# Four-layer graph network: adjacency products in a one-pass format behind a branch, the hyperedge sum one hyperedge at a time, x in DRAM

## The chip, the cores and the metric

The kernel runs on one core of one Trainium2 chip. The metric is the device time in microseconds (us) of one execution, and lower is better. The times given for a kernel are the median, the lowest and the highest of its runs. Besides these there is one execution under the hardware profiler; it has its own time and its own span, which is the time from the first to the last instruction. Engines are named as in the profile: PE is TensorE, DVE is VectorE, ACT is ScalarE, POOL is GpSimd, and SP is the engine that issues most of the transfers.

## The reference

The input x holds 8 batches of 2048 nodes with 64 features each. One adjacency matrix adj, 2048 x 2048 in fp32 with entries 0 and 1, is shared by all layers and batches. There are four layers, and each is x = x + layer(relu(layernorm(x))). H is 2048 nodes x 64 hyperedges, 0 or 1. What the layers compute, per batch:

```python
# layer 0: hypergraph attention and an adjacency mean
h = x @ W
s = leaky_relu(h @ a_node, 0.2)
alpha = softmax(where(H.T > 0, s[None, :], NEG), -1)       # 64 hyperedges x nodes
agg = alpha @ h                                            # 64 x 64 features
beta = sigmoid((h @ a_gn)[None, :] + (agg @ a_ge)[:, None])   # hyperedge x node
all_he = elu(beta[..., None] * h[None] + (1 - beta[..., None]) * agg[:, None])
industry = (adj / maximum(adj.sum(-1), 1)[:, None]) @ (x @ W_ind)
se = tanh(elu(agg) @ fcW + fcb) @ av                       # one score per hyperedge
coefs1 = softmax(where(H > 0, se[None, :], NEG), -1)       # node x hyperedge
g = einsum('ne,enf->nf', coefs1, all_he)                   # the sum over hyperedges
out = softmax-weighted mix of industry and g
# layer 1: Chebyshev terms x, A x, 2 A (A x) - x, with weights per node
#          from a 16-wide embedding
# layer 2: three times: effects = adj @ v; h = relu([v, effects] @ W1.T + b1);
#          v = h @ W2.T + b2
# layer 3: attention over all node pairs, scores multiplied by adj
```

The product adj @ something therefore occurs six times with all 8 batches side by side (512 columns): once in layer 0, twice in layer 1 and three times in layer 2.

## The kernel before

**Layouts.** Two batches of 64 features share the 128 partitions, so that an array is four tiles q = 0 to 3 of 128 x 2048 (features by nodes, "T form"), or sixteen tiles t of 128 nodes x 512 (batches and features, "node form"). `Halves` stores either form in two tiles with tags q0 to q7; a tag is one buffer of 2 MB (16 KB a partition), and an array that takes over a tag has to wait until the last reader of the former one is done. x itself stays in SBUF for the whole kernel as `self.x`, 4 MB, and `load_x` reads it from DRAM only in layer 0.

**Order.** The text is written in the order of the computation; the framework places semaphores and moves independent instructions of one engine past each other within what the buffers of the pools allow. All transfers of data are issued on SP in one queue, so that a transfer that has to wait for a buffer holds those behind it.

**Adjacency product** (`adj_product`, matmuls recorded under the helper `mm`, L57). Four chunks `ch` of 512 output nodes. In each, 16 source tiles m: a DMA brings two of them at once (`adj_t`, 512 KB), and for each of the four q one fp32 matmul of 128x128 by 128x512 adds to the accumulator `pp{q}` in PSUM. A chunk is 64 matmuls; `done` then empties the four accumulators. In layer 0 `each` adds up the rows of adj on GpSimd for the degree; in layer 1 `done` transposes the result back into node form, and `done2` runs the convolution (`pk`, `acc`, `po`); in layer 2 `done` runs the two small matrix products and the transposes (`to_nodes`).

**Sum over hyperedges** (`beta_and_weights`, then `hyper`). Partitions are (batch of the pair, hyperedge), and the loop runs over q and the 64 features f, 256 steps of 2048 nodes. h was split into three bf16 parts that were written to DRAM (`parts`) and come back as `mv`; `spread` copies one feature's row to all 128 partitions by matmuls with a 0/1 matrix `sel` into `pw`. `first_half` (L566, VectorE) forms z = (h - agg) * beta in two operations of 1024. `exponentials` (L574, L575, ScalarE) forms exp(z + agg) and relu(z + agg). `second_half` (L580, VectorE) forms y = min(exp, 1) + relu, which is elu plus 1, over 2048 columns, and four matmuls with `strip` sum y over the hyperedges with their weights `wt` into `acc`. `finish` collects the rows of a q.

**Layernorm** (`layernorm_relu`). Four chunks: a matmul with `center` subtracts the mean (`pc`, copied to `xc`), GpSimd squares, and two small matmuls give the variance (`pv`) and spread the inverse deviation (`pr`). `xc` has two buffers.

**Layer 3** (`attend`) has per batch and node tile an operation on GpSimd (L908) and two on VectorE (L911, L915) over 2048 columns, transposes (L928) and the product `po`.

## Time and profile before

| what | value |
|---|---|
| median of 3 runs | 5292.23 us (5259.44 to 5293.93) |
| the profiled execution, its time | 5293.93 us |
| its span | 5292.1 us |
| mean granted TensorE clock | 0.889 |
| busy: PE, PE weight loads | 4552.3 us (86%), 1832.7 us (35%) |
| busy: DVE, ACT, POOL | 2628.2 (50%), 1789.9 (34%), 945.0 us (18%) |
| DMA | 156.37 MB, mean 30 GB/s |

The order of the computation lets the span be cut into stages:

| stage | from, to (us) | length |
|---|---|---|
| start: layernorm, h, x_ind | 0 to 137.5 | 137.5 |
| layer 0, adjacency product | 137.5 to 386 | 248.5 |
| layer 0, attention of the hyperedges over nodes | 386 to 480 | 94 |
| layer 0, coefficients and sum over hyperedges | 480 to 1885 | 1405 |
| mix, layernorm of layer 1, transposes | 1885 to 2102 | 217 |
| layer 1, first product | 2102 to 2338 | 236 |
| layer 1, second product and convolution | 2338 to 3177 | 839 |
| layernorm of layer 2 | 3177 to 3253 | 76 |
| layer 2, three products | 3253 to 4055 | 802 |
| layer 3 | 4055 to 5292 | 1237 |

How to read the profile's lines. In the groups of instructions a line gives the source line, the engine, the operation, the tiles written and read, partitions x elements, and the number of instructions; then, after the bar, the busy time in us and the mean of one in ns; and after the second bar the engine's idle time just before them and what ended most of it. In the timeline a line gives the start in us, the duration in us, the engine, the line, the operation, its tiles and how many were joined in the line; in brackets stands the wait before it. In the table of windows a line gives the window, its length, and for each engine the busy time with the number of instructions, then the granted clock, the DMA share and the GB/s.

### The profile page before, as it was taken

How to read it: one execution, taken by the hardware profiler on the slowest of the kernel's cores; microseconds unless marked ns; L12 is line 12 of the kernel's file. 1: busy time of each engine (PE TensorE's matmuls, PEld its weight loads, DVE VectorE, ACT ScalarE, POOL GpSimd, SP SyncE). 2: the span in 40 equal slices, each digit the busy share in tenths (PEclk: the TensorE clock that was granted, in tenths of full speed). 3: DMA queues.
4: the chain of work that ended last, by engine and by line, in shares of the span. 5: the costliest groups of instructions: out<-in, count | busy, mean ns of one | idle time of the engine just before them, and what ended most of it. 6: DMA issues, size and time to landing. Idle time of an engine off the chain costs nothing.

```text
span 5292.1 us, 35768 instructions
## 1 busy us (share of the span) xinstructions
PE 4552.3 (86%) x14310; PEld 1832.7 (35%) x14374; DVE 2628.2 (50%) x2556; ACT 1789.9 (34%) x1652; POOL 945.0 (18%) x650
## 2 busy tenths in 40 slices
PE   8896566767566688999999999999999899999998
PEld 3333111111111122442323323444443455555555
DVE  3113898998989924003222232000002577777776
ACT  3002686886878832000000001000001244444444
POOL 4325000000000022004243241000001223232322
PEclk8997777677887788999999998999999798988898
DMA  2210000000000000230110101111110101010000
GB/s 81 92 56 0 3 6 5 5 5 5 6 3 0 0 24 28 72 100 12 48 25 24 32 0 57 60 63 64 61 64 16 40 5 36 5 36 5 28 5 5
DMA packets 76455, 156.37 MB, mean 30 GB/s; under 512 B 6464, under 2 KB 12736, under 8 KB 74112
## 3 DMA queue, kind: packets, MB, share of 16 engines
q1 hardware_dynamic: 76288, 154.07, 9.1%
q8 instruction: 113, 1.85, 0.1%
q14 instruction: 54, 0.44, 0.0%
HBM read 143.57 MB, written 10.49 MB: 29 GB/s over the span
## 4 chain that ended last, share of the span: by engine, by line
PE 56%; DVE 32%; POOL 7%; ACT 3%; issue 2%; DMA 1%; SPq 0%; POOLq 0%; DVEq 0%; ACTq 0%
PE pp L57 25%; DVE z_t L566 11%; PE po L57 9%; DVE e_t L580 7%; POOL acc L731 4%; PE pt L928 4%; PE p L57 4%; DVE e_x L580 3%; PE pd L57 3%; PE pk L57 3%; DVE m L915 3%; DVE y L730 2%; PE pr L57 2%; DVE m L911 2%; ACT m L920 1%
## 5 line engine op out<-in xcount | busy, mean ns | idle before, releaser
L566 DVE SCALAR_TENSOR_TENSOR z_t<-pw,agg_e,beta 128x1024 f32<-128x1024 f32 x512 | 636.9, 1279 | 38.1 <-PE pw L57 11.8
L575 ACT ACTIVATE z_t<-z_t,agg_e 128x2048 f32<-128x2048 f32 x256 | 512.7, 2003 | 8.2
L57 PE MATMUL po<-et,h_n 128*64 128x256 f32 x2048 | 511.6, 402 | 0.3 <-DVE st L919 0.3
L57 PE MATMUL pw<-mv,sel 128*128 128x512 bf16 x960 | 380.4, 497 | 120.3 <-DVE z_t L566 104.4
L57 PE MATMUL acc<-e_t,strip 128*32 128x512 f32 x1368 | 254.5, 810 | 232.5 <-DVE e_t L580 232.4
L57 PE MATMUL pp<-adj_t,v_a 128*128 128x512 f32 x1024 | 447.5, 592 | 0.0
L908 POOL TENSOR_SCALAR m<-ed,es 128x2048 f32<-128x2048 f32 x128 | 306.2, 2392 | 750.4 <-PE pt L928 421.7
L928 PE MATMUL pt<-ident,m 128*128 128x128 f32 x2048 | 357.6, 317 | 84.5 <-ACT m L920 50.2
L731 POOL TENSOR_TENSOR acc<-acc,y 128x512 f32<-128x512 f32 x224 | 282.7, 1262 | 814.6 <-DVE y L730 814.4
L574 ACT ACTIVATE e_t<-z_t,agg_e 128x2048 f32<-128x2048 f32 x171 | 342.4, 2002 | 181.2 <-DVE z_t L566 181.2
L580 DVE SCALAR_TENSOR_TENSOR e_t<-e_t,z_t 128x2048 f32<-128x2048 f32 x171 | 390.0, 2281 | 11.9 <-ACT z_t L575 11.9
L57 PEld LDWEIGHTS po<-et,h_n 128*64 128x64 f32 x2048 | 279.5, 144 | 195.4 <-issue 69.9
L915 DVE CUSTOM_DVE_ANT_0 m<-m,ar 128x2048 f32<-128x2048 f32 x128 | 345.7, 2701 | 2.2 <-POOL ar L873 2.2
L911 DVE SCALAR_TENSOR_TENSOR m<-ed,es,m 128x2048 f32<-128x2048 f32 x128 | 304.7, 2381 | 80.8 <-POOL m L908 80.8
L928 PEld LDWEIGHTS pt<-ident,m 128*128 128x128 f32 x2048 | 254.9, 158 | 256.2 <-ACT et L932 117.4
L932 ACT COPY et<-pt 128x512 f32<-128x512 f32 x384 | 215.2, 584 | 353.4 <-PE pt L928 353.0
L730 DVE TENSOR_TENSOR y<-pk,emb 128x512 f32<-128x512 f32 x224 | 154.8, 691 | 350.0 <-POOL acc L731 267.1
L63 ACT COPY xc<-pc 128x512 f32<-128x512 f32 x32 | 18.7, 585 | 914.4 <-PE pc L57 906.6
L920 ACT ACTIVATE m<-m,st 128x2048 f32<-128x2048 f32 x128 | 256.6, 2005 | 171.8 <-DVE st L919 171.8
L65 DVE COPY ef<-pp 128x512 f32<-128x512 f32 x24 | 16.6, 692 | 579.1 <-PE pp L57 567.6
L57 PEld LDWEIGHTS <-sel 128*128 128x128 bf16 x1024 | 98.2, 110 | 568.6 <-issue 530.5
L57 PE MATMUL pk<-x,w 64*128 64x512 f32 x512 | 286.8, 641 | 0.0
(250 smaller groups left out, 5441.1 us busy)
## 6 DMA issues: line engine op xcount, KB each, us to landing
adj_t<-in_adjT_dram SPq DMA_DIRECT2D x192, 512.0 KB
ar<-in_adj_dram SPq DMA_DIRECT2D x16, 1024.0 KB
xin<-in_xT_dram SPq DMA_DIRECT2D x8, 1024.0 KB
emb<-in_embT_dram SPq DMA_DIRECT2D x8, 1024.0 KB
parts<-part SPq DMA_DIRECT2D x16, 384.0 KB
mv<-parts SPq DMA_DIRECT2D x64, 96.0 KB
out_dram<-o SPq DMA_DIRECT2D x16, 256.0 KB
w<-in_wk_dram SPq DMA_DIRECT2D x6, 256.0 KB
```

The lines of the kernel that those rows point to most:

```text
L57: self.nc.tensor.matmul(out, lhsT, rhs, start=start, stop=stop)
L566: nc.vector.scalar_tensor_tensor(zs[i % 2][:, s], pws[i][c], agg_e[:, q, f : f + 1], beta(q)[:, s], op0=OP.subtract, op1=OP.mult,)
L574: nc.scalar.activation(es[i % 3], z, AF.Exp, bias=ag)
L575: nc.scalar.activation(z, z, AF.Relu, bias=ag)
L580: nc.vector.scalar_tensor_tensor(y, y, 1.0, zs[i % 2], op0=OP.min, op1=OP.add)
L730: nc.vector.tensor_mul(y, pk, emb[:, blk])
L731: nc.gpsimd.tensor_add(acc, acc, y)
L908: nc.gpsimd.tensor_scalar(m, ed, 0.2, es2[:, it, b : b + 1], op0=OP.mult, op1=OP.add)
L911: nc.vector.scalar_tensor_tensor(m, ed, es[:, it, b : b + 1], m, op0=OP.add, op1=OP.max)
L915: nc.vector.tensor_tensor_reduce(out=m, in0=m, in1=rows[i], op0=OP.mult, op1=OP.max, scale=1.0, scalar=-3.0e38, accum_out=st[:, 0:1],)
L920: nc.scalar.activation(m, m, AF.Exp, bias=st[:, 0:1], accum_out=st[:, 1:2])
L928: nc.tensor.transpose(pt[:, u], m[:, (t + u) * P : (t + u + 1) * P], ident)
```

## The change

The core of it:

```diff
+F12 = mybir.dt.float32r
...
+        dram = ctx.enter_context(tc.tile_pool(name="dram", bufs=1, space=bass.MemoryType.DRAM))
+        self.xs = [
+            [a["xT"][:, :, c * CW : (c + 1) * CW].rearrange("q p n -> p q n") for c in range(NC)]
+        ]
+        for i in range(3):
+            self.xs.append([dram.tile([P, NP, CW], F, name=f"x{i}_{c}") for c in range(NC)])
...
+    def exact(self, ap):
+        return ap.bitcast(F12) if self.short else ap
...
+    def split(self, dst, t, src, s=None):
...
+        self.nc.scalar.copy(hi.bitcast(F12), src)
+        self.nc.vector.tensor_sub(lo.bitcast(F12), src, hi)
...
+    def load_x(self, pool, layer, ch, bufs=None):
+        x = pool.tile([P, NP, CW], F, name="x_ch", bufs=bufs)
+        self.nc.sync.dma_start(x, self.xs[layer][ch])
+        return x
...
+    def store_x(self, layer, ch, x):
+        self.nc.sync.dma_start(self.xs[layer + 1][ch], x)
...
-                xc = w.tile([P, NP, CW], F, name="xc")
+                xc = w.tile([P, NP, CW], F, name="xc", bufs=1)
                 sq = w.tile([P, NP, CW], F, name="sq", bufs=1)
-                x = self.load_x(w, ch) if first else self.x[:, :, s]
+                x = self.load_x(w, layer, ch)
...
+                    moving = at[:, i]
+                    if self.short:
+                        moving = w.tile([P, CW], F12, name="adj_12", bufs=bufs)
+                        nc.scalar.copy(moving, at[:, i])
+                    for j, part in enumerate(src.parts):
+                        for q in range(NP):
+                            self.mm(
+                                out[q], self.exact(part(m)[:, q * P : (q + 1) * P]),
+                                moving,
+                                start=m == 0 and j == 0, stop=m == NT - 1 and j == 1,
+                            )
...
+    def check_adj(self, pool, slots):
...
+        nc, tc = self.nc, self.tc
+        rows = [slots.tile([P, 2, N], I32, name=f"rows{i}", tag=f"q{6 + i}") for i in range(2)]
+        seen = slots.tile([P, 2, N], I32, name="seen", tag="q8")
+        for t in range(NT):
+            row = rows[t // 2 % 2][:, t % 2]
+            nc.sync.dma_start(row, self.a["adj"][t * P : (t + 1) * P].bitcast(I32))
+            low = seen[:, 0] if t == 0 else row
+            nc.vector.tensor_scalar(low, row, LOW, None, op0=OP.bitwise_and)
+            if t > 0:
+                nc.vector.tensor_tensor(seen[:, 0], seen[:, 0], low, op=OP.bitwise_or)
...
+        top = pool.tile([P, 1], F, name="top")
+        nc.vector.tensor_reduce(top, seen[:, 0], axis=AX.X, op=OP.max)
+        flag = pool.tile([1, 1], I32, name="flag")
+        with tc.tile_pool(name="check_ps", bufs=1, space=PSUM) as ps:
+            pt = ps.tile([1, P], F, name="pt")
+            nc.tensor.transpose(pt, top, self.ident)
+            one = pool.tile([1, 1], F, name="one")
+            nc.vector.tensor_reduce(one, pt, axis=AX.X, op=OP.max)
+            nc.vector.tensor_scalar(flag, one, 0.0, None, op0=OP.is_gt)
+        return flag
...
+            self.layernorm_relu(0, write)
+            flag = self.check_adj(pool, slots)
...
+            with tc.tile_pool(name="h_ps", bufs=3, space=PSUM) as ps:
...
+        hn, h_t, h_n = self.h
...
+            w_ind = self.block_diag(k, a["W_ind"], "w_ind")
+            x_ind = Split(slots, "x_ind")
+            with tc.tile_pool(name="x_ps", bufs=3, space=PSUM) as ps:
+                for t in range(NT):
+                    pn = ps.tile([P, NP, P], F, name="pn")
+                    for q in range(NP):
+                        self.mm(pn[:, q], hn(q)[:, t * P : (t + 1) * P], w_ind)
+                    self.split(x_ind, t, pn.rearrange("n q f -> n (q f)"))
...
+            ind = Halves(slots, "ind", ("q0", "q1"), False)
...
+            beta = Halves(slots, "beta", ("q4", "q5"), False)
+            coef = Halves(slots, "coef", ("q6", "q7"), False)
...
+                for t in range(NT):
+                    mk = w.tile([P, 2, D], F, name="mk")
+                    nc.sync.dma_start(mk[:, 0], a["H"][t * P : (t + 1) * P])
...
+                    lg = w.tile([P, NB, D], F, name="lg")
+                    full = [P, NB, D]
+                    nc.gpsimd.tensor_mul(lg, se, mk[:, 0:1].to_broadcast(full))
+                    nc.gpsimd.tensor_add(lg, lg, mk[:, 1:2].to_broadcast(full))
+                    st = w.tile([P, 2, NB], F, name="st")
+                    nc.vector.tensor_reduce(st[:, 0], lg, axis=AX.X, op=OP.max)
+                    nc.vector.tensor_sub(lg, lg, st[:, 0].unsqueeze(2).to_broadcast(full))
+                    nc.scalar.activation(lg, lg, AF.Exp)
+                    nc.vector.tensor_reduce(st[:, 1], lg, axis=AX.X, op=OP.add)
+                    nc.vector.reciprocal(st[:, 1], st[:, 1])
+                    nc.vector.tensor_mul(lg, lg, st[:, 1].unsqueeze(2).to_broadcast(full))
...
+                        self.copy(coef.tiles[i][:, :, t * P : (t + 1) * P], pt[:, 2 * i : 2 * i + 2])
...
+            HW = 2 * CW
+            with (
+                tc.tile_pool(name="g", bufs=3) as w,
+                tc.tile_pool(name="g_ps", bufs=2, space=PSUM) as ps,
+            ):
+                for q in range(NP):
+                    acc = w.tile([P, N], F, name="acc", bufs=1)
+                    for e in range(D):
+                        pick = w.tile([P, 2, D], F, name="pick", bufs=2)
+                        nc.gpsimd.tensor_copy(
+                            pick, self.ident[:, e::D].unsqueeze(2).to_broadcast([P, 2, D])
+                        )
+                        pick = pick.rearrange("k s f -> k (s f)")
+                        ag = agg_t[:, q, e : e + 1]
+                        for c in range(N // HW):
+                            pb = ps.tile([P, HW], F, name="pb")
+                            pc = ps.tile([P, HW], F, name="pc")
+                            for pp, src in ((pb, beta), (pc, coef)):
+                                for i in range(2):
+                                    lo = c * HW + i * CW
+                                    self.mm(
+                                        pp[:, i * CW : (i + 1) * CW], pick, src(q)[:, lo : lo + CW]
+                                    )
+                            s = slice(c * HW, (c + 1) * HW)
+                            z = w.tile([P, HW], F, name="z")
+                            nc.vector.scalar_tensor_tensor(
+                                z, h_t(q)[:, s], ag, pb, op0=OP.subtract, op1=OP.mult
+                            )
+                            y = w.tile([P, HW], F, name="y")
+                            nc.scalar.activation(y, z, AF.Exp, bias=ag)
+                            nc.scalar.activation(z, z, AF.Relu, bias=ag)
+                            nc.vector.scalar_tensor_tensor(y, y, 1.0, z, op0=OP.min, op1=OP.add)
+                            if e == 0:
+                                nc.vector.tensor_mul(acc[:, s], y, pc)
+                            else:
+                                nc.vector.tensor_mul(y, y, pc)
+                                nc.gpsimd.tensor_add(acc[:, s], acc[:, s], y)
+                    nc.vector.tensor_scalar_add(h_t(q), acc, -1.0)
...
-                    xin = self.load_x(w, ch)
+                    x = self.load_x(w, 0, ch, bufs=2)
...
...
+        h_n = Split(slots, "h_n")
+        ah = Halves(slots, "ah", ("q4", "q5"), True)
...
+        ah_n = Split(slots, "ah_n")
+        for t in range(NT):
+            self.split(ah_n, t, ah(t))
...
+                two = slots.tile([P, 2, NP, CW], F, name="two", tag="q5")
+                x2, x = two[:, 0], two[:, 1]
+                nc.sync.dma_start(x, self.xs[1][ch])
...
+                self.store_x(1, ch, x)
+            self.adj_product(ah_n, w, ps, done2, bufs=3)
...
+        v_next = Halves(slots, "v_next", ("q2", "q3"), True)
...
+                v_n = Split(slots, "v_n")
+                for t in range(NT):
+                    self.split(v_n, t, v_next(t))
...
+                        x = self.load_x(w, 2, ch, bufs=1)
...
-                self.adj_product(bufs[step % 2], w, ps, done, bufs=6)
...
+                        self.store_x(2, ch, x)
...
+                self.adj_product(v_n, w, ps, done)
...
+                    x = self.load_x(w, 3, ic, bufs=1)
...
+                flag = kern.start(flags, slots)
+            long = tc.nc.values_load(flag, min_val=0, max_val=1)
...
+            with tc.If(long < 1) as check:
+                rest(True)
+            with check.Else():
+                rest(False)
```

**Products.** `short` is the arm of a branch in which `adj_product` copies each 512-column piece of adj on ScalarE into `adj_12`, of type float32r [...], and multiplies it by two parts of the features, `hi` (the features rounded by a ScalarE copy to that format) and `lo` (the rest, by a VectorE subtraction). A chunk then has 128 matmuls. `Split` holds the parts in q6 to q9. In the other arm adj stays fp32, and the two parts are multiplied as fp32.

**Check and branch.** `check_adj` reads all of adj as integers (16 transfers of 1 MB), keeps the low 12 bits of each (bitwise and), collects them (bitwise or), and forms a flag. The flag is read into registers, and layers 0 to 2 exist twice, in the two arms of `tc.If`. `start` (layernorm, check, h) stands ahead of the branch, the last layer behind it.

**Sum over hyperedges.** Partitions are now (batch of the pair, feature), as in T form, and the loop runs over q, hyperedges e and halves c of 1024 nodes: 512 half-steps. `pick` is built on GpSimd per (q, e); four fp32 matmuls with it spread the rows of beta (`pb`) and of the coefficients (`pc`). VectorE forms z from h_t (SBUF) and pb (PSUM), ScalarE forms exp and relu, VectorE forms y from two SBUF operands and multiplies it by pc, and GpSimd adds it to `acc` in SBUF. A new stage ahead of it ("coef") forms the softmax over hyperedges for each of the 16 node tiles and turns it into T form. `beta_and_weights` and `hyper`, the bf16 parts and their transfers are gone.

**x in memory.** `self.x` is gone; x lies in DRAM in four chunks a layer (`self.xs`), is loaded by `load_x` where it is used and stored by `store_x`. In `layernorm_relu` `xc` has one buffer. In layer 1 the second product has three buffers of adj_t instead of four, and `ah` keeps the first product in q4 and q5 until it is split. In layer 2 v_next takes q2 and q3, and adj_t has four buffers instead of six.

## The prediction

> **What bounds the kernel now.** I read the page's time slices, then a table of windows cut at the stages, then the chain of waits and the single instructions inside the two stages that change. The windows (us, then busy PE, weight loads, VectorE, ScalarE, GpSimd, clock, DMA share, GB/s):
>
> ```profile
> 137.50:386.00 248.50, 232.96 (x520) 101.92 (x520) 23.53 (x22) 0.00 (x0) 78.08 (x64) 0.96 0.24 74
> 480.00:1885.00 1405.00, 907.67 (x3375) 201.47 (x3439) 1243.11 (x875) 1039.33 (x534) 50.34 (x48) 0.76 0.01 4
> 2102.00:2338.00 236.00, 233.31 (x646) 104.94 (x645) 18.57 (x35) 14.87 (x33) 0.00 (x0) 0.98 0.25 75
> 2338.00:3177.00 839.00, 829.71 (x1664) 261.57 (x1664) 209.73 (x304) 0.00 (x0) 282.68 (x224) 0.99 0.10 29
> 3253.00:4055.00 802.00, 798.39 (x1944) 352.92 (x1942) 63.95 (x90) 55.06 (x88) 0.35 (x2) 1.00 0.18 59
> ```
>
> Lines 1, 3, 4 and 5 hold the six adjacency products (24 chunks): TensorE is busy nearly all the time and nothing else is. Line 2 is the sum over hyperedges: VectorE is full, TensorE is not. Inside these stages:
>
> ```profile
> L566 DVE SCALAR_TENSOR_TENSOR z_t<-pw,agg_e,beta 128x1024 f32<-128x1024 f32 x512 | 636.9, 1279 | 38.1 <-PE pw L57 11.8
> L580 DVE SCALAR_TENSOR_TENSOR e_t<-e_t,z_t 128x2048 f32<-128x2048 f32 x171 | 390.0, 2281 | 11.9 <-ACT z_t L575 11.9
> ...
> 3456.48 49.09 PE L57 MATMUL pp<-adj_t,v_a 128*128 128x512 f32 x114
> ...
> 700.58 0.59 PE L57 MATMUL pw<-mv,sel 128*128 128x512 bf16 x2 [0.32 <-DVE z_t L566]
> ...
> 4613.88 2.29 DVE L915 CUSTOM_DVE_ANT_0 m<-m,ar 128x2048 f32<-128x2048 f32 x1
> 4641.72 3.63 DVE L915 CUSTOM_DVE_ANT_0 m<-m,ar 128x2048 f32<-128x2048 f32 x1
> ...
> 4641.24 1.97 POOL L908 TENSOR_SCALAR m<-ed,es 128x2048 f32<-128x2048 f32 x1 [7.69 <-issue]
> ```
>
> An fp32 product is two MATMUL records; 114 of them in 49.09 us is 0.429 each, 0.858 a product. Two bf16 ones end in 0.59 although each lasts 0.377, so one pass takes 0.213. The last three lines matter most below: a VectorE operation with two SBUF inputs takes 2.29 us alone and 3.63 when a GpSimd operation holds until 4643.21; it then ends 2.1 us after GpSimd.
>
> [...]The pitch of 0.429 against a load of 0.190 (the LDWEIGHTS row of pp) agrees for the products; in the convolution it does not wholly: pairs start 1.055 apart instead of 0.858. [...]the masks row shows 1226 ns for 2048 elements, L580 2281.[...]
>
> **The change, part by part**, against the profiled execution (5293.9 us, span 5292.1; the runs' median is 5292.2). The taken arm is the short one, since adj holds zeros and ones only.
>
> *Products.* A chunk is 64 fp32 products (54.9 us); it becomes 128 one-pass ones. No row shows this format at 4 bytes. I take the bf16 pitch: 128 x 0.214 = 27.4, saving 27.5. [...]an uncovered load adds 0.1 (half of the convolution's 0.2 a product), and two passes would make it 0.429. ScalarE's new copies of adj (16 x about 0.6 = 9.6 a chunk), GpSimd's row sums (16 x 1.26 = 20.2) and DMA (4.2 MB in 27 us, 155 GB/s; 148 was moved in 98 to 137 us at a share of 0.45) stay under 27.4. By stage:
> - First layer: 4 x (27.4 + 6.0 at each boundary, the 3.36 us reciprocal and what surrounds it) = 134 for 248.5: -115.
> - Second layer, first product: 4 x (27.4 + 3 of transposes + about 2 until the four accumulators are emptied) + 2 = 132 for 236: -104.
> - Second product: 4 x 27.5 = -110. The split of ah frees q4, on which the embedding load waits on SP, and adj_t stands behind it there: +9. Sum -101.
> - Third layer: a chunk of 67.2 becomes 27.4 + 12 fp32 products (10.3) + 16 transposes (2.0) + 1.1 of waits for hh, which the built order fills with three to six one-pass matmuls. 12 x 40.8 + 3 splits begun late at 4 = 502 for 802: -300.
>
> *Sum over hyperedges.* 256 steps over features become 512 half-steps over hyperedges of 1024 columns. VectorE per half-step: z 1279 (the same operand kinds as L566), y 2281 - 1067 = 1214, the product with pc 691 + 533 = 1224 (512 columns more at 0.96 a ns): 3.72, or 3.47 when each overlaps its predecessor by 0.085, as L566's pairs do. TensorE: four fp32 products, 3.43. ScalarE: two of about 1.12. GpSimd: the add lies between 1262 (512) and 4513 (2048 columns, L299), 2.35, plus half a pick (a copy of 512 takes 0.61; about 0.3), together 2.5. The built order keeps VectorE two half-steps deep (y, the z two ahead, the product), so ScalarE's 2.3 us are covered. But y has two SBUF inputs and the add reads SBUF: 1.2 + 2.35 + 0.15 = 3.7 exclude one another. Three resources thus lie between 3.4 and 3.7; coupled in fixed order none is met exactly. Behind a held y stand z and the product on VectorE, and behind these TensorE's next pb and pc, which wait for the PSUM that they free. I take 3.8: 512 x 3.8 = 1946, plus 24 for four ends (the single acc must be drained, then one 2048 operation). Bounds: 3.47 (lock wholly hidden) and 4.22 (loads uncovered, 4 x 1.055).
> Before it, the coefficient stage: 16 tiles of about 3.8 us VectorE (four 128x512 operations of 0.69, 0.42 of copies, 0.6 small), 61, with GpSimd's 2 x 1.26 a tile in conflict with two of them, and 10 to fill: 78. Sum 2048 for 1405: +643.
>
> *Check, branch, start.* Sixteen ands (1.23 to 2.28 each), fifteen ors (2.29) and a reduction (2.28) are 56 to 73 us of VectorE among the 31 of the layernorm[...]. The layernorm's end moves from 79 to about 115; 16.8 MB more DMA fits beside it. The flag's short chain 5, then h 32 (32 us of TensorE, held behind the flag's transpose), [...]loads of w_ind behind it 5, x_ind 17: the product starts at 179, not 137.5: +42. The bf16 parts and their DMAs are gone, and this is inside that figure.
>
> *x in memory.* The loads after the mix wait on SP behind the last store: +10. Third layer's layernorm +3. Leaving the arm and reloading before the last layer +15. Elsewhere loads run 30 us ahead, and cost 7 (a 1 MB load took 5.2) where that cover is gone. xc has one buffer instead of two, so a chunk's first copies wait until the chunk before has read its last xc: 0 to 10 us a layernorm, by the 76 us that four chunks take now; I take 6 in each of these three.
>
> Sum: 42 - 115 + 643 + 16 - 104 - 101 + 9 - 300 + 21 = +111. 5293.9 + 111 = 5405.
>
> **Rivals.** A measurement of this kernel can tell about 1% from no change.
> - A, as summed: 5405, own range 5328 to 5518 (half-step 3.65 to 4.0). Chance 0.47. For it: the lock line above. Against: 3.47 is possible.
> - B, faster: the add runs exactly under z and the product, which have one SBUF input each, so the lock costs nothing and VectorE streams. Half-step 3.47: -169, 5236. It decides when z and the product (2.35) are as long as the add and y always asks first. The convolution speaks for it: y there (one SBUF input) takes 691 with and without the add beside it. Chance 0.17.
> - C, TensorE bounds the loop: pick's loads stay uncovered as in the convolution, 4.22: +215, 5620. Against: all tiles are 128x128, as in the products. Chance 0.13.
> - D, the lock the other way round: the add asks first, y waits for it whole, then z and the product run with GpSimd idle: 2.35 + 1.0 + 2.35 = 5.7. If a quarter of the half-steps do so, +243, 5648; all, +973, 6378. Against: y stands directly behind the product on VectorE, the add waits for its semaphore. Chance 0.08.
> - E, the format doesn't do what it says: 0.1 more per matmul, 24 x 128 x 0.1 = +307, 5712; two passes, 24 x 27.5 = +660, 6065. Chance 0.15.
>
> **How the numbers follow.** The likeliest case gives 5405. Range 5210 to 5735: it takes in B, C and E's first half and leaves out some 0.2. Faster by over 1% (below 5239): somewhat over half of B, and A where several of the other stages fall short, 0.15. Within 1%: B's rest and the low end of A, 0.15. Slower: 0.70.
>
> **What would show it.** In the profile after: one-pass pp records of about 0.38 with a pitch of 0.214, chunks of the third layer 41 apart; z, y and acc starting 3.8 apart, y longer than 1.21 and the add longer than 2.35 in some; the first product at about 179 and the mix at about 2455. Wrong if the pitch is over 0.25, if a half-step leaves 3.6 to 4.0, or if a stage outside these moves by over 20.

## The result, and the profile after

The changed kernel takes 5526.15 us (median of 4 runs, 5523.31 to 5539.47) against 5292.4 us: a ratio of 1.0462, 95% interval 1.0418 to 1.0506, so it is slower. The forecast was 5405, slower, with a range of 5210 to 5735. Direction and range hold; the loss is 234 us where 111 were summed, so the size does not hold. The profiled execution took 5524.61 us with a span of 5522.7 us; the differences below are of spans.

The stages, cut in the same way as before. The border between the two products of the second layer is put at the convolution's first matmuls in both kernels (2337.8 and 2812.5 us).

| stage | before | after | change | the prediction's term |
|---|---|---|---|---|
| start | 137.5 | 158.8 | +21 | +42 |
| first layer, product | 248.5 | 151.8 | -97 | -115 |
| attention of the hyperedges | 94 | 92.1 | -2 | 0 |
| coefficients and sum over hyperedges | 1405 | 2021.8 | +617 | +643 |
| mix, layernorm, transposes | 217 | 230.3 | +13 | +16 |
| second layer, first product | 236 | 157.7 | -78 | -104 |
| second product and convolution | 839 | 870.9 | **+32** | **-101** |
| layernorm of the third layer | 76 | 86.8 | +11 | +9 |
| third layer, products | 802 | 501.7 | -300 | -300 |
| last layer with what leads to it | 1237 | 1250.8 | +14 | +21 |
| sum | 5292 | 5522.7 | +231 | +111 |

One row is off by 133 us. The others are off by 13 together, the other way; that is in part luck, since four of them are off by 18 to 26 each and cancel in pairs. The windows that answer to those of before (window, length, busy PE, weight loads, VectorE, ScalarE, GpSimd, clock, DMA share, GB/s):

```profile
158.80:310.60 151.80, 130.04 (x520) 101.26 (x521) 28.57 (x26) 37.21 (x60) 64.91 (x52) 0.93 0.31 97
402.70:2424.50 2021.80, 1864.07 (x4192) 776.57 (x4192) 1929.08 (x1667) 1215.16 (x1082) 1598.91 (x791) 0.98 0.00 1
2654.80:2812.50 157.70, 150.74 (x721) 114.16 (x721) 35.26 (x72) 67.27 (x134) 0.00 (x0) 0.90 0.40 120
2812.50:3683.40 870.90, 854.06 (x1664) 287.14 (x1665) 209.41 (x304) 39.36 (x64) 283.02 (x224) 0.83 0.13 38
3770.20:4271.90 501.70, 498.22 (x1973) 352.10 (x1971) 91.20 (x133) 193.80 (x323) 0.28 (x2) 1.00 0.34 113
```

In the fourth line TensorE is as full as before (854 of 871 us), but the clock is 0.83 instead of 0.99. Cut finer, at the last of the four convolution chunks, with the timeline around the cut (start, duration, instruction, count, wait before it):

```profile
3340.00:3397.00 57.00, 56.38 (x179) 30.88 (x177) 11.40 (x17) 8.07 (x13) 11.40 (x9) 1.00 0.38 111
3397.00:3399.20 2.20, 0.10 (x1) 0.00 (x0) 2.14 (x5) 0.00 (x0) 0.00 (x0) 0.76 0.00 0
3399.20:3674.40 275.20, 272.91 (x274) 65.22 (x274) 45.44 (x66) 0.00 (x0) 70.71 (x56) 0.50 0.00 0
...
3392.41 1.07 PE L106 MATMUL pp<-adj,ah_n_lo 128*128 128x512 f32 x4
3393.31 3.79 PE L106 MATMUL pk<-q,w 128*128 128x512 f32 x8
3399.23 21.26 PE L106 MATMUL pk<-q,w 128*128 128x512 f32 x21 [2.13 <-DVE acc L647]
```

TensorE runs at full clock to 3397, stops for 2.13 us, and then works at half clock for 275 us with one pause of 2.26 at its end, which the kernel before has too. From its first product to its last the chunk of the convolution takes 281 us (3393.3 to 3674.4) where it took 155 (3019.9 to 3174.5). So 126 of the 133 us lie here, 2 of them in the stop and the rest in the clock. The stop can be read from the traces. After a chunk's product VectorE forms x2 in eight operations (5.7 us) before it reaches the first product with emb, which frees one of three pk buffers. In the kernel before, x2 began at 3017.5, while the last fp32 matmuls ran on to 3019.9, and three pairs of the convolution (a pair is the product with w01 and the one with w2 that add up in one pk) filled the time to 3026; the product with emb came at 3023.2. Now the one-pass matmuls end 0.5 us after x2 begins, two of the six products of those pairs already stand further up in the built order, the other four end at 3397.1, and the product with emb comes at 3398.5. In the chunks ahead the next chunk's product fills the hole. Of the four products that end at 3397.1 three are those with w2, which use 64 rows (two records for each product):

```profile
L106 PE MATMUL pk<-q,w 64*128 64x512 f32 x6 | 2.8, 606 | 0.0
```

The groups of the page that carry the rest:

```profile
L509 POOL TENSOR_TENSOR acc<-acc,y 128x1024 f32<-128x1024 f32 x504 | 1437.3, 2869 | 23.0 <-DVE y L508 22.8
L106 PE MATMUL pb<-q,pick 128*128 128x512 f32 x2048 | 1000.1, 606 | 103.5 <-POOL pick L482 102.0
L504 DVE SCALAR_TENSOR_TENSOR y<-y,z 128x1024 f32<-128x1024 f32 x512 | 699.5, 1366 | 5.4 <-ACT z L503 5.2
L235 ACT CAST adj<-adj_t 128x512 fp32r<-128x512 f32 x384 | 238.0, 621 | 887.0 <-PE pp L106 861.0
```

On average y takes 1.37 us instead of 1.21 and the addition 2.87 instead of 2.35 (the shortest takes 2.34), which looks like the exclusion that the prediction made its likeliest case. The second line says something else: TensorE waits 102 us for pick. Which of the two holds the loop is asked below. ScalarE's copies of adj (0.62 us each) wait for TensorE, not the reverse.

### The profile page after: what moved, and what is told of

Its sections match the earlier page's. It is cut to its first block, busy times and chain, and to the rows that moved or that the text cites. A ratio compares the mean times of both kernels' runs of the same rounds, so it can differ in the third digit from the quotient of the medians.

```text
span 5522.7 us, 42055 instructions
## 1 busy us (share of the span) xinstructions
PE 5030.7 (91%) x15111; PEld 2425.8 (44%) x15111; DVE 3423.0 (62%) x3462; ACT 2219.5 (40%) x2632; POOL 2475.9 (45%) x1363
## 4 chain that ended last, share of the span: by engine, by line
PE 44%; POOL 31%; DVE 12%; issue 8%; ACT 3%; DMA 1%; POOLq 0%; SPq 0%; ACTq 0%; DVEq 0%
POOL acc L509 24%; PE pp L106 13%; PE po L106 7%; PE pk L106 7%; PE pt L857 4%; PE p L106 3%; POOL acc L651 3%; PE pd L106 3%; DVE m L844 3%; POOL pick L482 2%; PE pr L106 2%; DVE y L650 2%; DVE m L840 2%; ACT m L849 1%; PE pc L106 1%
## 5 line engine op out<-in xcount | busy, mean ns | idle before, releaser
L509 POOL TENSOR_TENSOR acc<-acc,y 128x1024 f32<-128x1024 f32 x504 | 1437.3, 2869 | 23.0 <-DVE y L508 22.8
L106 PE MATMUL pb<-q,pick 128*128 128x512 f32 x2048 | 1000.1, 606 | 103.5 <-POOL pick L482 102.0
L106 PE MATMUL pc<-coef,pick 128*128 128x512 f32 x2048 | 962.8, 593 | 6.8 <-DVE acc L506 6.2
L502 ACT ACTIVATE y<-z,agg_t 128x1024 f32<-128x1024 f32 x512 | 588.3, 1149 | 745.4 <-POOL acc L509 706.8
L504 DVE SCALAR_TENSOR_TENSOR y<-y,z 128x1024 f32<-128x1024 f32 x512 | 699.5, 1366 | 5.4 <-ACT z L503 5.2
L498 DVE SCALAR_TENSOR_TENSOR z<-q,agg_t,pb 128x1024 f32<-128x1024 f32 x512 | 651.8, 1274 | 64.1 <-PE pb L106 64.1
L106 PE MATMUL pk<-q,w 128*128 128x512 f32 (+1 forms) x1024 | 658.5, 762 | 7.4 <-DMA w<-in_wk_dram 5.1
L508 DVE TENSOR_TENSOR y<-y,pc 128x1024 f32<-128x1024 f32 x504 | 610.1, 1211 | 0.1
L106 PEld LDWEIGHTS pc<-coef,pick 128*128 128x128 f32 x2048 | 388.7, 190 | 499.8 <-issue 449.8
L503 ACT ACTIVATE z<-z,agg_t 128x1024 f32<-128x1024 f32 x512 | 588.1, 1149 | 16.7
```

The source lines that it names most:

```text
L106: self.nc.tensor.matmul(out, lhsT, rhs, start=start, stop=stop)
L498: nc.vector.scalar_tensor_tensor(z, h_t(q)[:, s], ag, pb, op0=OP.subtract, op1=OP.mult)
L502: nc.scalar.activation(y, z, AF.Exp, bias=ag)
L503: nc.scalar.activation(z, z, AF.Relu, bias=ag)
L504: nc.vector.scalar_tensor_tensor(y, y, 1.0, z, op0=OP.min, op1=OP.add)
L508: nc.vector.tensor_mul(y, y, pc)
```

## Experiments: the half clock

Two theories stood at the start. *Gap*: the stop of 2.13 us brings the half clock, and the convolution can hold a full clock but not regain it. *Load*: the long dense work ahead, 1,940 us of it in the new sum, brings it, wherever TensorE then is.

**x2 later in the last chunk.** The stop is taken away.

```diff
+                end = ch == NC - 1
+                for q in range(NP if not end else 1):
+                    second(q)
                 for q in range(NP):
+                    if end and q > 0:
+                        second(q)
                     po = ps.tile([P, CW], F, name="po")
```

> The changed kernel, with one edit: in the last chunk of the second product of layer 1 the VectorE operations that form x2 for q = 1 to 3 stand each ahead of their own q instead of all ahead of the convolution, so that VectorE reaches the first product with emb some 4 us earlier. Theory gap (a stop of TensorE of 2.13 us at 3397 us brings the half clock, and the convolution can't lift it again): the stop goes, the clock stays at 1.00 to the end of the stage, the last chunk's convolution takes 155 us as in the kernel before instead of 275, and the time is 5526 - 120 = 5405. Rival load (the clock is cut after a long time of dense work, wherever TensorE then is): the cut comes all the same, time 5520 to 5530.

Measured: 5399.57 us, ratio to the kernel before 1.0229 (1.0192 to 1.0267). The clock in the stretch that was at half:

```profile
3399.20:3530.00 130.80, 129.75 (x248) 34.89 (x246) 39.87 (x58) 0.00 (x0) 60.08 (x48) 1.00 0.00 0
```

Gap holds, load falls: the new sum is untouched in this kernel. Without the half clock the sum of the prediction, 5405, is met within 6 us, with the luck of the cancelling rows named above.

**The same stop in the kernel before.** Eight copies ahead of x2 in the last chunk.

```diff
+                if ch == NC - 1:
+                    for i in range(8):
+                        nc.vector.tensor_copy(x2[:, 0], out[0])
```

> The kernel before, with eight VectorE copies of 128x512 (0.69 us each) put ahead of x2 in the last chunk of layer 1, so that TensorE has to stop for 2 to 4 us between the last product and the convolution. Theory gap: the clock falls to half there although none of the change is in this kernel, the last chunk's convolution takes 270 us instead of 155, time 5292 + 120 = 5412. Rival load: the stop costs itself and no more, 5295 to 5300, clock 1.00 throughout.

Measured: 5405.61 us. The timeline and the window of this run:

```profile
3028.52 5.48 PE L57 MATMUL pk<-x,w 64*128 64x512 f32 x6 [5.23 <-DVE x L717]
...
3028.00:3305.00 277.00, 276.44 (x278) 66.76 (x278) 46.80 (x68) 0.00 (x0) 69.38 (x55) 0.50 0.00 0
```

A stop of 5.23 us costs about 119 us (5405.61 against 5286.41 for the kernel before, run beside it) in a kernel that has nothing of the change. So the half clock does not come from the change as such; after a stop the kernel before shows it too, and by itself it had no such stop here.

**A dense burst in the middle.** Sixteen fp32 products after the first q of the last chunk.

```diff
+                    if ch == NC - 1 and q == 0:
+                        sc = ps.tile([P, CW], F, name="sc", tag="pp0")
+                        for i in range(16):
+                            self.mm(sc, ident, x[:, 0], start=i == 0, stop=i == 15)
+                        nc.vector.tensor_copy(x2[:, 0], sc)
```

> The changed kernel with 16 dense fp32 products (128x128 by 128x512, the form of the adjacency products before) issued once after the first q of the last chunk's convolution; they add 14 us at full clock and 28 at half. Theory gap with a hold that differs from a lift: the half clock comes at 3397 as before, ends within the burst, and does not come back: of 275 us for the last chunk about 80 stay at half clock, time about 5526 - 90 + 20 = 5456. Rival load: the clock stays at half or falls back to half right after the burst, time 5526 + 28 = 5554.

Measured: 5455.71 us. Before, in and after the burst:

```profile
3397.80:3465.60 67.80, 67.73 (x69) 16.17 (x69) 11.58 (x18) 0.00 (x0) 17.66 (x14) 0.50 0.00 0
3465.60:3481.00 15.40, 15.40 (x34) 6.92 (x34) 0.69 (x1) 0.00 (x0) 1.26 (x1) 0.90 0.00 0
3481.00:3595.00 114.00, 110.81 (x209) 29.36 (x207) 34.02 (x50) 0.00 (x0) 51.72 (x41) 0.98 0.00 0
```

The clock is back at 1.00 about 3 us into the burst (0.90 over these 15.4 us), and in the convolution behind it it stays high to the end of the stage (0.98 over 114 us). So in this run the convolution kept 0.50 before the burst and nearly 1.00 after it: that much of the theory is shown.

**All matmuls of the convolution with 128 rows.** Each pair was one matmul of 128 rows and one of 64.

```diff
-            w2 = k.tile([P, DO], F, name="w2")
+            w2 = k.tile([P, 2, DO], F, name="w2")
+            nc.vector.memset(w2, 0.0)
             for j in range(2):
-                nc.sync.dma_start(w2[j * D : (j + 1) * D], a["wk"][2])
+                nc.sync.dma_start(w2[j * D : (j + 1) * D, j], a["wk"][2])
...
-                            self.mm(pk, w2[h, c], x2[h, q], start=False)
+                            self.mm(pk, w2[:, half, c], x2[:, q], start=False)
```

> The changed kernel with the 64-row weight w2 of the convolution padded with zero rows to 128, so that both matmuls of each pair take 128 rows; the stop of TensorE before the last chunk is left as it is (emb_d and y lose one buffer each to make room). Theory gap, in the form that the lift depends on how many rows of the array the matmuls use: the clock comes back within some 10 us of the stop, the last chunk takes about 165 us, time 5526 - 110 = 5416. In the form that it depends on the time between matmuls alone (weights that load uncovered): the half clock stays, time 5520 to 5535. Rival load: the same, half clock, 5520 to 5535.

Measured: 5334.39 us, 82 below the forecast, because more changed than was meant. From the timeline, sixteen products in the changed kernel, sixteen here, and the stop here:

```profile
2868.73 16.94 PE L106 MATMUL pk<-q,w 128*128 128x512 f32 x32
...
3350.08 14.00 PE L106 MATMUL pk<-q,w 128*128 128x512 f32 x32
3336.97 10.57 PE L106 MATMUL pk<-q,w 128*128 128x512 f32 x24 [2.11 <-DVE acc L648]
...
3336.90:3464.00 127.10, 120.97 (x273) 48.46 (x274) 45.48 (x67) 0.00 (x0) 70.80 (x56) 1.00 0.00 0
```

(The first two lines join 32 records each, two for each fp32 product, so they hold eight pairs of products.) A pair takes 1.71 us, not 2.11: where 128 and 64 rows alternate, a product took some 0.2 us more, about the 0.19 us that the traces show for one weight load. And after a stop of 2.11 us the clock did not fall in this run.

**The padding in the kernel before**, to measure it without a half clock.

> The kernel before with w2 padded to 128 rows (emb_d and y lose one buffer each). There is no half clock here to take away, so the padding shows alone: 512 fp32 products at 0.857 instead of 1.055 us, 101 us less, 5185. Rival (VectorE and GpSimd bound the convolution, or the pitch isn't due to the rows): 5270 to 5300.

Measured: 5207.23 us, ratio 0.9853 (0.9808 to 0.9899). The padding gains 84 us by itself where 101 were expected; of the 17 that are missing, 12 are a longer wait for the last addition of each acc (0.54 us instead of 0.15, 32 times).

**Rows, or the share of time in which TensorE streams?** The padding raised both. The next kernel puts a 64-row matmul of two columns into each pair.

```diff
+                            self.mm(pk[:, :2], w2[lo, 1, c], x2[lo, q, :2], start=False, stop=False)
                             self.mm(pk, w2[:, half, c], x2[:, q], start=False)
```

> The changed kernel with w2 padded to 128 rows, and in every pair of the convolution a small 64-row matmul of two columns with zero weights between the two large ones. All streaming then uses 128 rows, as in the padded kernel, but each change of the row count should leave a weight load uncovered again, so that a pair takes some 2.1 to 2.3 us and TensorE streams 75 to 80 % of the time, as in the changed kernel. Theory rows (what holds or loses the clock after the stop is how many rows the matmuls use): the clock stays at 1.00 after the stop of 2.1 us, time 5400 to 5450. Rival share (it is the share of time in which TensorE streams): half clock from the stop to the end of the stage, 5530 to 5580. If a pair stays at 1.71 us, the uncovered load does not come from the change of rows, and the time is near 5334.

Measured: 5442.99 us, clock 1.00, but this does not decide: its pairs had grown to 2.22 us and so covered most of the stop, which was only 0.82 us. It does show again that pairs were longer where the rows change (2.22 us against 1.71). Repeated with a stop:

> The kernel before this one (w2 padded, small 64-row matmuls in each pair) with three VectorE copies of 0.69 us between x2 and the first product with emb in the last chunk, since its stop was only 0.82 us and so the clock was not put to the test. The stop becomes 2.9 us. Theory rows: the clock stays at 1.00 or comes back within 10 us, time 5445 to 5460. Rival share: half clock from the stop to the end of the stage (pairs of 2.22 us becoming about 4), 5443 + 130 = 5573.

Measured: 5451.63 us. The stop and the clock behind it:

```profile
3421.26 15.21 PE L106 MATMUL pk<-q,w 128*128 128x512 f32 x36 [1.54 <-DVE acc L653]
...
3420.00:3424.00 4.00, 2.74 (x5) 1.30 (x6) 3.19 (x6) 0.00 (x0) 1.26 (x1) 0.71 0.00 0
3424.00:3428.00 4.00, 4.00 (x10) 1.50 (x8) 1.48 (x3) 0.00 (x0) 2.54 (x2) 0.86 0.00 0
3440.00:3480.00 40.00, 39.93 (x104) 15.96 (x104) 11.76 (x17) 0.00 (x0) 17.68 (x14) 1.00 0.00 1
```

The clock falls at the end of a stop of 1.54 us and is back some 3.4 us later (the shares 0.71 and 0.86 make 2.3 and 1.1 us at half clock), with pairs of 2.22 us that stream 77% of the time (1.71 of 2.22). In the changed kernel a pair at half clock takes 4.01 us, of which four records of 0.86 us (twice 0.43) are 3.43, or 85%, and the clock does not come back. So the share of time did not decide here. What these runs leave is the rows in use: with 128 rows the clock came back, in the alternation of 128 and 64 rows it did not in 275 us. The stage ahead fits: in the first chunk of layer 1, where 64-row transposes alternate with one-pass matmuls, the clock stays at 0.50 until 2678, 4 us after the last of the transposes.

**Dense 128-row pairs after a longer stop.**

> w2 padded to 128 rows with the pairs dense (1.71 us), and four such copies in the last chunk, so that the stop grows from 2.11 to 4.9 us. The clock should fall to half in such a stop. If dense pairs of 128 rows can lift it again, it is back within 4 to 10 us and the time is 5334 + 3 + 5 = 5342; if nothing in the convolution can, 5334 + 130 = 5464.

Measured: 5341.95 us, as forecast, but not for the reason forecast: the stop was 2.84 us and the clock stayed at 1.00. Stops of 2.11 and 2.84 us left it in these two padded kernels, stops of 1.54 and 2.13 us did not elsewhere; the length alone does not tell.

The traces tell more. In the kernel before and in the changed one all changes of the granted clock (315 and 135) lie on one grid with steps of 3.41 us (within 0.01 us). And two other padded kernels of this study, described below (three picks and padding, old sum and padding), have the stop of 2.11 us too, with the same products around it, and there the clock does fall, for one step. Cut in steps of this length, the step before the fall in the changed kernel; the step with most of the stop of 2.84 us; three steps of three picks and padding (stop from 3217.13 to 3219.24); two of the old sum and padding (stop from 2770.73 to 2772.84):

```profile
3394.74:3398.15 3.41, 2.36 (x6) 0.75 (x4) 3.34 (x6) 0.00 (x0) 0.00 (x0) 1.00 0.00 0
...
3336.99:3340.40 3.41, 1.51 (x4) 0.38 (x2) 3.32 (x6) 0.00 (x0) 0.00 (x0) 1.00 0.00 0
...
3217.00:3220.42 3.42, 1.31 (x4) 0.68 (x4) 3.32 (x6) 0.00 (x0) 0.56 (x1) 1.00 0.00 0
3220.42:3223.83 3.41, 3.41 (x5) 1.35 (x4) 0.69 (x1) 0.00 (x0) 2.96 (x3) 0.50 0.00 0
3223.83:3227.24 3.41, 3.41 (x9) 1.52 (x8) 1.39 (x2) 0.00 (x0) 1.54 (x2) 1.00 0.00 0
...
2769.72:2773.13 3.41, 1.30 (x4) 0.47 (x3) 3.34 (x6) 0.00 (x0) 0.00 (x0) 1.00 0.01 2
2773.13:2776.55 3.42, 3.42 (x5) 1.36 (x5) 0.92 (x3) 0.00 (x0) 2.53 (x2) 0.50 0.00 0
```

In these two kernels the 2.11 us lie within one step, of which TensorE was busy for 1.31 and 1.30 us, and the clock falls at its end; in the step of the stop of 2.84 us it was busy for 1.51, and the clock stayed. In the first padded kernel (stop from 3334.86 to 3336.97) it stayed too; that the grid divided that stop is the author's estimate. So padding did not prevent the fall in these two; after one step the clock was back. In the changed kernel a stop of only 1.05 us in the step was enough, and all six records in the rest of it used 64 rows.

An estimate from the records of two traces, the kernel before from 1885 to 4055 us and the changed one from 2424 to 4271 (1,175 steps), counts a record of 512 columns as 0.429 us (the pitch in the prediction), a one-pass one as 0.227, others by their columns, twice that at half clock, up to the record's end, times its rows over 128, as a share of the step. The 19 steps before a fall reach at most 0.38; the 997 that kept the full clock hold 0.38 or more. Of the 138 steps at half clock that stayed so none is above 0.75 (0.70 in the changed kernel's convolution, where up to 95% of a step was streaming), and the 21 before a rise hold 0.69 or more. In these two traces rows times time thus tells the steps apart almost wholly, and time alone does not; no run was made to test where the borders lie.

## Experiments: the sum over hyperedges

The loop took 1942 us against 1970, the coefficient stage ahead of it 80 against 78. The forecast gave the exclusion of y and the addition as the reason.

**No addition.**

```diff
-                                nc.gpsimd.tensor_add(acc[:, s], acc[:, s], y)
```

> The changed kernel without the GpSimd addition to acc for e above 0, so that the sum holds the first hyperedge only; everything else of the half-step stays. Theory lock (y and the add exclude one another): y returns to 1.21 us, the half-step to 3.47, the loop from 1942 to about 1785, time 5526 - 157 = 5369. Rival TensorE (four fp32 products at 0.857 and the wait for pick): half-step 3.75, 5510 to 5525.

Measured: 5519.75 us, where the expectation was 5369. The loop takes 1942.1 us with the addition and 1942.0 without. The page's lines:

```profile
L106 PE MATMUL pb<-q,pick 128*128 128x512 f32 x2048 | 999.7, 606 | 112.4 <-POOL pick L482 112.4
L504 DVE SCALAR_TENSOR_TENSOR y<-y,z 128x1024 f32<-128x1024 f32 x512 | 623.4, 1218 | 0.4
```

y is back at 1.22 us and nothing is gained in the loop: the reason was wrong. TensorE still waits for pick. In the changed kernel's timeline:

```profile
1303.51 0.29 POOL L482 COPY pick<-ident 128x128 f32<-128x128 f32 x1 [1.61 <-PE pc L106]
1303.86 1.98 PE L106 MATMUL pb<-q,pick 128*128 128x512 f32 x4 [0.41 <-POOL pick L482]
```

pick has two buffers. The built order runs pb two half-steps, one hyperedge, ahead of pc, so the buffer for the next pick is released by the last pc of the hyperedge before, and this is the moment at which TensorE needs it. It stops 0.41 us, and two hyperedge halves take 7.54 us (1303.86 to 1311.40) where eight products need 6.87 (8 x 0.858).

**Three buffers for pick**, with the addition, without it, and with the padding:

> The changed kernel with three buffers for pick instead of two. Theory pick (with two buffers GpSimd can only make the next pick when the last product with the one before last has ended, just when TensorE needs it, so TensorE stops 0.4 to 0.5 us per hyperedge and refills, 0.67 in all): the stop goes, the half-step falls from 3.77 to what TensorE or VectorE needs, 3.43 to 3.5, the loop from 1942 to about 1780, time 5526 - 160 = 5366. Rival lock (y and the GpSimd add exclude one another and hold the half-step at 3.7 by themselves, so that taking away one of two equal bounds shows nothing): 5490 to 5526.

> Three buffers for pick and no GpSimd addition to acc for e above 0 (the sum then holds the first hyperedge only). Both theories: half-step 3.43 to 3.5, time 5345 to 5375. What lies between this and the run with the addition is what the exclusion of y and the addition costs once pick no longer hides it: nothing if theory pick is all, 0.2 to 0.3 us a half-step (100 to 150 us) if the lock binds too.

> The changed kernel with both small edits, three buffers for pick and w2 padded to 128 rows. If the two gains add, 5334 - 160 = 5174, which is less than the kernel before; if the lock holds the half-step, 5300 to 5334.

| kernel | time (us) | loop (us) | per half-step |
|---|---|---|---|
| changed | 5526.15 | 1942.1 | 3.79 |
| no addition | 5519.75 | 1942.0 | 3.79 |
| three picks | 5421.56 | 1822.3 | 3.56 |
| three picks, no addition | 5376.99 | 1783.5 | 3.48 |
| three picks and padding | 5218.8 | 1822.0 | 3.56 |

(The loop is taken from the first pb to the first matmul of the mix, in one profiled execution of each; the last column is a 512th of it.) The pick buffer is worth 120 us of loop. The kernel as a whole gains 105 of them; in the profiled executions the last layer, which both kernels share, took 1267.6 us instead of 1250.8. Below the pick buffer lies the addition, worth 39 us (3.56 to 3.48). Of these, y's longer time, the direct mark of the exclusion, is 20 us (1.256 against 1.216, 512 times), and 10 are waits for the last addition at the four ends of q; the rest is not assigned. With three picks the page shows which side waits:

```profile
L509 POOL TENSOR_TENSOR acc<-acc,y 128x1024 f32<-128x1024 f32 x504 | 1638.8, 3252 | 80.7 <-DVE y L508 78.6
L504 DVE SCALAR_TENSOR_TENSOR y<-y,z 128x1024 f32<-128x1024 f32 x512 | 643.3, 1256 | 5.8 <-ACT z L503 5.6
```

The addition takes 3.25 us where its shortest took 2.34, and y 1.256 against 1.216 without the addition: it is the addition that is stretched, as the forecast's rival B assumed. In the timeline an addition that begins at 1301.44, while y runs from 1301.22 to 1302.52, ends at 1304.75, which is 2.2 us after y. The last kernel, the change with two small edits, takes less time than the kernel before: ratio 0.9877 (0.9817 to 0.9937).

## Experiments: the change without its new sum

The products, the check, the branch and x in memory, with the sum over hyperedges of the kernel before:

```diff
+        self.parts = [dram.tile([P, 3, N], BF, name=f"parts{q}") for q in range(NP)]
...
+        mv = [slots.tile([P, 4, N], BF, name=f"mv{i}", tag=f"q{8 + i}") for i in range(2)]
...
+            self.beta_and_weights(slots, k, h_t, agn, ge, wt, mask)
+            self.hyper(slots, self.parts, h_t, agg_e, wt)
```

> The products, check, branch and x in memory of the changed kernel with the sum over hyperedges of the kernel before (its bf16 parts made in the start, its mv in the two buffers that hold the low part of x_ind during the product). Theory gap: the sum over hyperedges costs +617 us in the changed kernel's trace and the stop before the last convolution chunk is still there, so half clock there and 5526 - 617 + about 10 for the parts = 4919. Rival load (the clock is cut because the new sum keeps TensorE dense for 1940 us): no half clock, 4795.

> The same with w2 padded to 128 rows. Theory: the padded pairs keep their weight loads under the matmuls (pair 1.71 instead of 2.11 us) and the stop no longer lowers the clock; they took 192 us from the changed kernel and take the same here: 4727. If the gain were bound to the state of the clock in that run: 4795 to 4900.

Measured: 4952.37 us, ratio 0.9376 (0.934 to 0.9412), and with the padding 4744.81 us, ratio **0.8981** (0.8941 to 0.9022), the fastest complete kernel of the study (4727 was expected). The first has the stop and the half clock too, though its sum over hyperedges leaves TensorE far from full (907.67 of 1405 us in the kernel before); that is the second piece of evidence against *load*:

```profile
2821.75 24.11 PE L109 MATMUL pk<-q,w 128*128 128x512 f32 x24 [2.13 <-DVE acc L830]
...
2900.00:2950.00 50.00, 50.00 (x51) 12.06 (x50) 8.11 (x12) 0.00 (x0) 12.63 (x10) 0.50 0.00 0
```

It is 33 us above what was expected. In its trace the first product starts at 183.0 us instead of 158.8, which is 24 of them; that the bf16 parts, which stand in the start beside the check, are the reason was not tested.

**The last kernel without the check's transfers and operations**; the flag is set to 0, so it holds for an adj of zeros and ones alone, and the branch stays:

> Products with the old sum and w2 padded, without the check's 16 transfers, ands, ors and reductions: the flag is set to 0 by a memset, so that the kernel only holds for an adj of zeros and ones; the branch stays. By the stage table the start became 21 us longer with check, branch and reordering: 4745 - 21 = 4724. Rival (the branch and the loads behind it are what costs, the check hides beside the layernorm): 4740 to 4750.

Measured: 4730.08 us, ratio 0.8966 (0.8918 to 0.9013), which its interval does not separate from the 0.8981 with the check. In the traces the first product starts at 158.7 instead of 182.8 us, so 24 us in one execution of each.

## Why the prediction was right or wrong

- **Wrong: the term of the second product (-101, measured +32).** The step that failed is "Second product: 4 x 27.5 = -110": it took the convolution behind each product as unchanged. The shorter product uncovered x2 in the last chunk, TensorE stopped 2.13 us, and the half clock behind it cost some 124 us. The prediction named an uncovered load and PSUM as what could come late, but followed no stop into the clock, although its own window of before showed the convolution at 0.99 and nothing had shown what a stop does there. No rival held this case. It is nearly the whole error: with the stop removed the time is 5399.57 against 5405.
- **Right in size, wrong in reason: the loop.** 1942 against 1970. The half-step of 3.8 was argued from the exclusion of y and the addition, and the coupling of three nearly equal resources was a guess on top. That 3.79 came out is luck. The runs show the turn of the pick buffer at 3.79, the addition under it at 3.56, and 3.48 without both; 3.47 was the bound given for an exclusion (the prediction's lock) that costs nothing. VectorE's pace of 0.96 columns a ns, on which the sizes of y and the product rest, is in the traces: 2281 ns for 2048 columns (L580) and 1218 for 1024 (L504 without the addition). The prediction counted pick as a copy of 0.3 us on an engine with time to spare and did not ask when its buffer is handed back.
- **First product of layer 1 (-104, measured -78).** The transposes and the start of the first chunk run at half clock until 2678 us, which no term held; and 5.1 us go to a load of the convolution's weights that now comes late.
- **One-pass matmuls.** One lasts 0.389 us and four start 0.907 apart, 0.227 each where 0.214 was taken from bf16; in the first layer four start 0.933 apart at a clock of 1.00, which stays unexplained. Rival E (0.1 more, or two passes) is out: the pitch is 0.013 above the one taken, not 0.1. Most chunks of the third layer start 41.9 us apart (forecast 41), and the stage is met exactly.
- **Start (+42, measured +21).** The first product starts at 158.8, not 179. The flag is there at 112 (115 + 5 were taken), h ends at 141, the first matmul behind the branch starts at 142.6 after a wait of 1.1, where branch and loads were put at 10 (for the branch an estimate of the author's that no run had shown), and x_ind takes 16.
- **x in memory** fits: +13, +11 and +14 for +16, +9 and +21. The last of these is weak evidence, since the last layer, with the same instructions, took from 1251 to 1274 us in kernels that differ only ahead of it.
- **A slip in a sum, without weight here:** with half-steps of 4.0 case A ends at 5405 + 102 = 5507, not at 5518. And the 1.055 us that the prediction gives for pairs is the distance of two products, each a pair of records.

## What to carry to other kernels

When a change makes one stage of TensorE shorter, look at what its tail covered: a stop of 2.13 us was followed here by 275 us at half clock, and the work behind it did not bring the clock back; the table of windows with the clock column finds it at once. Where matmuls of 64 and 128 rows alternate, try to pad the short ones with zero rows; here a pair took 1.71 us for 2.11, and after stops of 2.11 and 2.84 us the clock either stayed or was back in one step of 3.41 us. When two resources are equal, take one away before naming it as the bound, and count when a small helper tile's buffer comes back, not only what the helper costs.

## What was not expected of the hardware

Behind a stop of 2.13 us TensorE was at half clock for 275 us in which it hardly paused, and 3 us of dense matmuls ended it. In the two traces that were cut in steps every change of the clock lay on a grid of 3.41 us, and a stop of 2.11 us lowered the clock in two padded kernels and left it at 1.00 in a third. Rows counted, not only time: steps of the changed kernel's convolution that streamed up to 95% of the time, with 64 rows in about half of the records, stayed at half clock. Where the row counts alternated a product took 0.2 us more than with equal ones (2.11 us a pair against 1.71). The format at 4 bytes is one record for 512 columns, with 0.227 us from one to the next, against two records and 0.858 us for an fp32 product.
